# A graph network kernel: the last group's scatters spread between chunks, and the first chunks' fetches moved, in its second layer

## The chip, the cores and the metric

One core of a Trainium2 chip runs the whole program in one launch. The core has five engines with queues of their own: TensorE (PE: matmuls; PEld is its loading of weights), VectorE (DVE), ScalarE (ACT), GpSimd (POOL) and SyncE (SP), which here only starts transfers. The metric is the device time of one execution in microseconds (us), lower is better. All data are 32-bit floats.

## The reference

The model is a stack of four layers, each `x = x + layer(relu(layernorm(x)))`, on x of 128 x 64 x 256. Layer 0 is two graph convolutions and an LSTM, layer 2 a convolution with two batch norms, layer 3 a dense graph attention. The change lies in layer 1, an attention over 512 edges of a graph with 64 nodes and 4 heads:

```python
Xq = (H @ W_lin.T).reshape(bt, n, h, dh)
Xv = (H @ W_val.T).reshape(bt, n, h, dh)
Qs = Xq[:, src]
Kt = Xq[:, dst]
e = jnp.einsum('behd,hd->beh', jax.nn.leaky_relu(Qs + Kt, LRELU_SLOPE), a)
e = e + jnp.log(A0[src, dst] + EPS)[None, :, None]
...
attn = ex / denom[src]
...
Y = jax.ops.segment_sum(attn[..., None] * Vt, src, num_segments=n)
...
return Y @ W_out.T
```

The softmax runs over the edges that share a source node.

## The kernel before

The 8192 tokens (128 x 64) are cut into 16 chunks of 512 (`NCH`), and these into 4 groups of 4 chunks (`NGR`; a group is 2048 tokens). Layer 1 runs in two stretches.

The edge loop, `edges(q)` for q from 0 to 31, takes two tiles of 128 tokens per step: `gather` (line 959) forms query sums for all edges with a matmul, ScalarE copies them out of the accumulation banks, VectorE applies the leaky ReLU (971), `project` (940) makes the queries and values of the tiles to come, `score` (974) adds each edge's score into the group's bank. A group has its scores after eight steps. Its softmax, `edge_softmax(g)` (990), is a generator. `step_behind` (1171) advances it by one `yield`, and `edges` calls this three times per step, so that a group's softmax is spread over some six steps of the next group.

The parts of `edge_softmax`, in order: scores plus log weights (993), two scans for the maximum (996, 998), subtraction and exponential (1002, 1003), two scans for the sums (1006, 1008), four reciprocals (1013), the product (1015), four transposes on TensorE (1019), the multiplication by `twins` into `attn` (1024). Then eight scatters from GpSimd (1058), one for each half of the partitions (`par`) and block of 128 edges (`ec`), write rows of attention to a field of 64 x 64 in DRAM. `part_back` (1039) brings the field back into the tile `dense[g]`, in two loads or, for the last group, in four.

From step 25 on, every second step also calls `values_of(n)` (1188) for n = 0 to 3. Behind the loop it runs for n = 4 to 15 (1285), and this is the second stretch, the chunk loop. `values_of(n)` calls `weigh(n)` (64 small matmuls of 64 x 64, line 1122, and a copy on ScalarE), `fetch(n + 2)` (values `xv` from DRAM, but for the last four chunks, which stay on chip; and the chunk `xo` of x), `turn_attention(n + 2)` (one copy of `dense` on ScalarE and one on VectorE, line 1104), the store of chunk n - 2, and `put_out(n - 1)` (16 matmuls, line 1142, and two additions to x, 1152). Unless `hold` is set it then calls `sums` (1156) for chunks that are put out: sums for the next layer's norm on VectorE, and four small operations on GpSimd for the roots. For n = 0 it first fetches and turns chunks 0 and 1. Chunks 12 to 15 are those of the last group, so chunk 12's attention (`LAST`) is turned only at n = 11.

The last group's softmax has no edge steps left to hide behind. Four parts of it run at the end of step 31, seven ahead of n = 4, and the rest, from the transposes on, in one go ahead of n = 6.

The order in each engine's queue is set at build time by a scheduler that may move an instruction ahead of others that it takes to be ready later. `late(ins)` pins an instruction behind the one traced before it on its engine. `add_manual_dep` with `Sync` makes an instruction wait for another one.

Buffers that matter: four accumulation banks (`bank`), two double banks (`pair_bank`), three `att`, three `xv`, four `xo`, four of each small statistics tile. `l1` is the layer's scope.

Of the kernel before, what the change touches and what calls it, by code (L numbers as in the profile page):

```python
# [12 lines left out]
AF = mybir.ActivationFunctionType  # L13
ALU = mybir.AluOpType
# [16 lines left out]
def gnn_stack_kernel(ctx: ExitStack, tc: tile.TileContext, a: dict, out: bass.AP):  # L31
# [11 lines left out]
    def bank():  # L43
        return psums["now"].tile([P, 512], F32, tag="bank", name="bank", bufs=psums["banks"])
# [26 lines left out]
    def late(ins):  # L71

        tc.keep_in_program_order(ins)
# [805 lines left out]
    with ExitStack() as l1:  # L879
# [110 lines left out]
        def edge_softmax(g):  # L990

            e = e1.tile([P, E], F32, tag="e", name="e")
            late(nc.vector.tensor_tensor(e, scores[g], logw, ALU.add))
            run = e1.tile([P, E], F32, tag="run", name="run")
            yield
            late(nc.vector.tensor_tensor_scan(run, first, e, NEG, ALU.add, ALU.max))
            yield
            late(nc.vector.tensor_tensor_scan(
                run[:, ::-1], final[:, ::-1], run[:, ::-1], NEG, ALU.add, ALU.max
            ))  # L1000
            yield
            late(nc.vector.tensor_tensor(e, e, run, ALU.subtract))
            late(nc.scalar.activation(e, e, AF.Exp))
            yield

            late(nc.vector.tensor_tensor_scan(run, keep, e, 0.0, ALU.mult, ALU.add))
            yield
            late(nc.vector.tensor_tensor_scan(
                run[:, ::-1], final[:, ::-1], run[:, ::-1], NEG, ALU.add, ALU.max
            ))  # L1010
            yield
            for k in range(NE):
                late(nc.vector.reciprocal(run[:, k * P : (k + 1) * P], run[:, k * P : (k + 1) * P]))
                yield
            late(nc.vector.tensor_tensor(e, e, run, ALU.mult))
            yield
            p = bank()
            for ec in range(NE):
                ins = nc.tensor.transpose(p[:, ec * P : (ec + 1) * P], e[:, ec * P : (ec + 1) * P], ident)
                if ec == 0 and g == NGR - 1:  # L1020
                    late(ins)
            yield
            attn = e1.tile([P, NE, P], F32, tag="attn", name="attn")
            late(nc.vector.tensor_tensor(
                attn,
                p.rearrange("p (e r) -> p e r", e=NE),
                twins.unsqueeze(2).to_broadcast([P, NE, P]),
                ALU.mult,
            ))

            sent = [[], []]

            dense[g] = attp.tile([P, T, T], F32, tag="dense", name="dense")

            def bring_back(par, parts=1):
                for k in range(parts):
                    part_back(par, k, parts)

            def part_back(par, k, parts):

                r, s = slice(par * T, (par + 1) * T), slice(k * 32 // parts, (k + 1) * 32 // parts)
                back = nc.gpsimd.dma_start(
                    out=dense[g][r, :, :].rearrange("p (o s) r -> p o s r", o=2)[:, :, s, :],
                    in_=fields1[2 * g + par][: T * T, :].rearrange("(t o s) r -> t o s r", t=T, o=2)[
                        :, :, s, :
                    ],
                )
                for ins in sent[par]:
                    tc.add_manual_dep(
                        back.ins,  # L1050
                        ins.ins.name,
                        mybir.DependencyInfo(mybir.DependencyClass.Sync, mybir.DependencyReason.DATA),
                        reason="rows of the field",
                    )

            for par in range(2):
                for ec in range(NE):
                    ins = nc.gpsimd.indirect_dma_start(
                        out=fields1[2 * g + par][:, :],
                        out_offset=bass.IndirectOffsetOnAxis(ap=row_of[:, ec : ec + 1], axis=0),  # L1060
                        in_=attn[:, ec, par * T : (par + 1) * T],
                        in_offset=None,
                    )
                    for earlier in sent[par]:
                        tc.declare_no_dep(ins.ins, earlier.ins, reason="different rows")
                    sent[par].append(ins)
                    if ec % 2:
                        yield
            if g == NGR - 1:

                for k in range(2):
                    for par in range(2):
                        part_back(par, k, 2)
            else:
                bring_back(0)
                yield
                bring_back(1)
# [33 lines left out]
        def weigh(n):  # L1111

            (xv, xt), att = fetched.pop(n), turned.pop(n)
            yT = yp.tile([P, 8, 2, T], F32, tag="yT", name="yT")
            p = pair_bank()
            for c in range(2):
                for i in range(4):
                    for h2 in range(2):
                        for par in range(2):
                            r = slice(par * T, (par + 1) * T)  # L1120
                            hd = 2 * c + h2
                            ins = nc.tensor.matmul(  # L1122
                                p[h2 * T : (h2 + 1) * T, par, (c * 4 + i) * T : (c * 4 + i + 1) * T],
                                xv[r, i, hd * T : (hd + 1) * T],
                                att[r, i % 2, i // 2 * 4 + hd, :],
                                start=True,
                                stop=True,
                            )
                            if c + i + h2 + par == 0:
                                late(ins)  # L1130
            nc.scalar.copy(
                yT.rearrange("p k o t -> p o k t"), p.rearrange("p o (k t) -> p o k t", t=T)
            )
            return xt, yT
# [18 lines left out]
            stores.append((n, xt))  # L1153
            unnormed.append((n, xt))

        def sums(n, xt):

            st = stat.tile([P, 4, 6], F32, tag="ln_st", name="ln_st")
            mv = stat.tile([P, 4, 2], F32, tag="ln_mv", name="ln_mv")
            for i in range(4):  # L1160
                nc.vector.bn_stats(st[:, i, :], xt[:, i, :])
                nc.vector.bn_aggr(mv[:, i, :], st[:, i, :])
            rs, nm = x_rs[:, n, :], x_nm[:, n, :]
            nc.gpsimd.tensor_scalar(rs, mv[:, :, 1], 1e-5, None, ALU.add)
            nc.gpsimd.tensor_tensor(rs, rs, half_power, ALU.pow)
            nc.gpsimd.tensor_tensor(nm, mv[:, :, 0], rs, ALU.mult)
            nc.gpsimd.tensor_scalar(nm, nm, -1.0, None, ALU.mult)
# [14 lines left out]
                step_behind()  # L1182

        NT = NTOK // P
        dense, fetched, turned, weighed, stores, unnormed = {}, {}, {}, [], [], []
        LAST = NCH - 4

        def values_of(n, hold=False):

            if n == 0:  # L1190
                for k in range(2):
                    fetch(k)
                    turn_attention(k)
            one = (n, *weigh(n))
            if n + 2 < NCH:
                fetch(n + 2)
            if n == LAST:
                turn_attention(n + 1)
            if n + 2 < NCH and not LAST <= n + 2 < LAST + 2:
                turn_attention(n + 2)  # L1200
            flush_stores()
            flush_values()

            if n + 1 == LAST:
                turn_attention(LAST)
            weighed.append(one)
            if not hold:
                while unnormed:
                    sums(*unnormed.pop(0))

        def flush_stores():
            while stores:
# [7 lines left out]
        def next_score():  # L1220
            q, c, lrs = waiting.pop(0)
            score(q, c, lrs)
            if q % 8 == 7 and c == 1:
                behind.append(edge_softmax(q // 8))

        def edges(q):
# [20 lines left out]
                sums1(n + 3, (0, 1))  # L1247
            while len(waiting) > (1 if q < NT // 2 - 1 else 0):
                next_score()

        coming1 = {n: load_x1(n) for n in (2, 3)}
        hTs[0] = t1.tile([P, 2, CHUNK], F32, tag="hT1", name="hT1")
# [32 lines left out]
        for n in range(4, NCH):  # L1285
            if n == 4:
                for _ in range(7):
                    step_behind()
            if n == 6:
                finish_behind()  # L1290
            values_of(n, n in (4, 5))
            if n - 10 in first_x2:
                scale_x(n - 10, first_x2.pop(n - 10))
        flush_stores()
# [631 lines left out]
```

## Time and profile before

| what | us |
|---|---|
| median of 3 runs | 2091.2 (2090.15 to 2093.34) |
| the profiled execution | 2088.75 |
| its span | 2086.8 |
| layer 1 in it, about | 1300 to 1697 |
| its edge loop, about | 1308 to 1619 |
| its chunk loop (chunk 4 on) | 1624 to 1695 |

The profile shows one execution. Its page gives each engine's busy time and share of the span, the busy share in 40 slices, and the clock that TensorE was granted. Views of the trace give more: the chain of waits follows the work that ended last back from its end; the timeline lists instructions in order of time, with the idle time before them and what ended it; the windows give busy time by stretch. "issue" is time in which an engine waited for nothing that the profile shows. On GpSimd, DMA_INDIRECT is a scatter and DMA_DIRECT2D a plain transfer.

### The profile page before, as it was taken

The page shows a single profiled execution, that of the slowest core. Times are in us where ns is not written, and L with a number is a line of the kernel's source. Part 1 is how long each engine was busy: PE and PEld are TensorE (multiplying, and loading weights), DVE is VectorE, ACT ScalarE, POOL GpSimd, SP SyncE. Part 2 cuts the span into 40 slices and gives each one's busy share as a digit, 9 for nine tenths or more (in the row PEclk, how much of TensorE's full clock was granted, in tenths as well). Part 3 has the DMA queues.
Part 4 walks back from the last instruction along what each step waited for, and adds up shares of the span by engine and source line. Part 5 has one row for each costly group of instructions (what it writes and reads, how often), then busy time and mean ns, then how long its engine had stood idle before and what let it go on. Part 6 is the DMA issues. An engine that isn't in the chain of part 4 may idle for free.

```text
span 2086.8 us, 25504 instructions
## 1 busy us (share of the span) xinstructions
PE 2016.4 (97%) x9444; PEld 1353.1 (65%) x9444; DVE 1362.5 (65%) x2509; ACT 1180.1 (57%) x2222; POOL 317.7 (15%) x422
## 2 busy tenths in 40 slices
PE   8999999999999999999999998999999999999998
PEld 6776488766688746886667885333334775444786
DVE  8764766564655577557446555676766767786776
ACT  4344766554555467566546553666665356592444
POOL 3000010100200020002001002114322420000563
PEclk9999999999999999999999999999999999999899
DMA  9331000100100250001001006113234851023012
GB/s 310 98 96 51 0 21 1 41 0 1 41 1 1 89 194 21 1 1 41 1 0 41 1 1 227 61 51 96 75 82 117 257 186 59 0 71 91 31 61 71
DMA packets 94461, 135.06 MB, mean 65 GB/s; under 512 B 6401, under 2 KB 82049, under 8 KB 92161
## 3 DMA queue, kind: packets, MB, share of 16 engines
q1 hardware_dynamic: 87616, 109.11, 15.9%
q0 software_dynamic: 6112, 24.12, 3.9%
q8 instruction: 74, 1.21, 0.2%
q14 instruction: 51, 0.41, 0.1%
q10 hardware_dynamic: 608, 0.20, 0.1%
HBM read 87.28 MB, written 46.14 MB: 64 GB/s over the span
## 4 chain that ended last, share of the span: by engine, by line
PE 85%; DVE 7%; ACT 3%; DMA 2%; issue 1%; POOL 1%; SPq 0%; ACTq 0%; POOLq 0%; DVEq 0%
PE pa L643 25%; PE pc L643 13%; PE bank L50 12%; PE pb L643 6%; PE pa L1361 5%; PE pair L964 5%; PE bank L948 5%; PE bank L1142 3%; PE bank L980 2%; PE pc L1361 2%; PE pb L1361 1%; PE pair L50 1%; ACT gate L671 1%; PE pair L1122 1%; PE bank L167 1%
## 5 line engine op out<-in xcount | busy, mean ns | idle before, releaser
L643 PE MATMUL pa<-xop,sih 128*128 128x256 f32 (+2 forms) x1056 | 343.9, 417 | 11.3 <-DVE gate L697 7.7
L671 ACT ACTIVATE gate<-gate,bias 128x256 f32<-128x256 f32 (+2 forms) x368 | 247.4, 679 | 172.4 <-DVE gate L687 89.1
L643 PEld LDWEIGHTS pa<-xop,sih 128*128 128x128 f32 x1056 | 198.2, 190 | 86.6 <-issue 22.2
L643 PE MATMUL pc<-xop,wih 128*128 128x256 f32 (+2 forms) x736 | 251.2, 423 | 0.0
L687 DVE TENSOR_TENSOR gate<-pb,gate 128x256 f32<-128x256 f32 (+2 forms) x184 | 87.4, 475 | 224.3 <-PE pb L643 152.6
L643 PE MATMUL pa<-lstm_h,shh 128*128 128x256 f32 (+1 forms) x672 | 212.7, 398 | 0.0
L971 DVE SCALAR_TENSOR_TENSOR lr<-lr 128x1024 f32<-128x1024 f32 x128 | 150.3, 1217 | 64.5 <-ACT lr L970 58.3
L643 PEld LDWEIGHTS pc<-xop,wih 128*128 128x128 f32 x736 | 139.8, 190 | 51.2 <-issue 23.0
L702 DVE TENSOR_TENSOR gate<-pc,gate 128x256 f32<-128x256 f32 (+2 forms) x184 | 87.6, 476 | 119.5 <-PE pc L643 119.2
L970 ACT COPY lr<-pair 128x1024 f32<-128x1024 f32 x128 | 123.1, 1013 | 48.8 <-PE pair L964 46.2
L643 PEld LDWEIGHTS pa<-lstm_h,shh 128*128 128x128 f32 x672 | 127.7, 190 | 30.2
L643 PE MATMUL pc<-lstm_h,whh 128*128 128x256 f32 (+1 forms) x448 | 141.8, 398 | 0.0
L686 ACT COPY gate<-pa 128x256 f32<-128x256 f32 (+2 forms) x184 | 76.0, 413 | 96.2 <-PE pa L643 95.8
L964 PE MATMUL pair<-sd_hot,xq 64*128 64x512 f32 x512 | 128.0, 618 | 2.3 <-ACT lr L970 2.3
L948 PE MATMUL bank<-wlv,hT 128*128 128x512 f32 x256 | 118.4, 605 | 0.2 <-ACT hT L156 0.2
L697 DVE TENSOR_TENSOR gate<-pa,gate 128x256 f32<-128x256 f32 (+2 forms) x184 | 87.3, 475 | 44.0 <-PE pa L643 43.4
L691 ACT COPY gate<-pa 128x256 f32<-128x256 f32 (+2 forms) x184 | 75.5, 410 | 59.0 <-PE pa L643 57.6
L671 ACT ACTIVATE gate<-pa,bias 128x256 f32<-128x256 f32 (+2 forms) x184 | 93.9, 510 | 25.9 <-PE pa L643 24.3
L434 POOL TENSOR_TENSOR sih<-wih 128x512 f32<-128x512 f32 x8 | 10.6, 1325 | 626.1 <-DMA wih<-in_WihT 438.9
L643 PE MATMUL pa<-xop,wih 128*128 128x256 f32 (+1 forms) x320 | 101.4, 398 | 2.6 <-ACT xop L624 2.6
L643 PE MATMUL pb<-xop,wih 128*128 128x256 f32 (+1 forms) x320 | 100.3, 398 | 0.4 <-DVE gate L687 0.4
L643 PEld LDWEIGHTS pc<-lstm_h,whh 128*128 128x128 f32 x448 | 85.1, 190 | 20.1
(337 smaller groups left out, 3824.4 us busy)
## 6 DMA issues: line engine op xcount, KB each, us to landing
field<-sd_hot SPq DMA_DIRECT2D x8, 1152.0 KB, 11.2
wih<-in_WihT SPq DMA_DIRECT2D x8, 1024.0 KB, 6.4
xres<-in_x SPq DMA_DIRECT2D x16, 512.0 KB, 5.5
xa<-xres POOLq DMA_DIRECT2D x16, 512.0 KB
xin<-xb SPq DMA_DIRECT2D x16, 512.0 KB, 3.9
h<-xb SPq DMA_DIRECT2D x16, 512.0 KB, 3.9
xin<-in_x SPq DMA_DIRECT2D x15, 512.0 KB, 7.0
out_x<-h SPq DMA_DIRECT2D x15, 512.0 KB, 2.9
```

Of the source, the lines that this page charges most:

```text
L50: nc.tensor.matmul(o, lhsT, rhs, start=start, stop=stop)
L643: ins = nc.tensor.matmul(p[:, : self.N], weights[kind, self.phase](k, q), x[k], start=first_ and kind == "ih", stop=kind == "hh" or not se ...
L671: nc.scalar.activation(out, in_, AF.Tanh if q == 2 else AF.Sigmoid, bias=bias[:, self.w - 1, 2 * q + j : 2 * q + j + 1],)
L686: nc.scalar.copy(blk[0, 0], pa[:, :N])
L687: nc.vector.tensor_tensor(blk[0, 0], pb[:, :N], blk[0, 0], ALU.add)
L697: nc.vector.tensor_tensor(blk[1, 1], pa[:, :N], blk[1, 1], ALU.add)
L702: nc.vector.tensor_tensor(blk[1, 0], pc[:, :N], blk[1, 0], ALU.add)
L948: ins = nc.tensor.matmul(p, hTs[n][:, k, i * P : (i + 1) * P], wlv[:, k, :], start=k == 0, stop=k == 1)
L964: ins = nc.tensor.matmul(p[:, par, :], queries[it][r, c * P : (c + 1) * P], sd_hot[r, :], start=True, stop=True)
L970: nc.scalar.copy(lr, p)
L971: nc.vector.scalar_tensor_tensor(lr, lr, 0.2, lr, ALU.mult, ALU.max)
L1361: ins = nc.tensor.matmul(p, lhs[k], x[k], start=first_, stop=last_one, skip_group_check=True)
```

## The change

The softmax of groups 0 to 2 gets one more step between product and transposes, and its transposes are pinned. For the last group, the multiplication by `twins` moves from one VectorE operation to four on ScalarE, one for each block of 128 edges; transposes and multiplication form one step, and the scatters follow in batches of three, three and two, each scatter waiting for the last matmul of the latest weighting (`last_weigh`). The four loads of the last group's field are pinned behind the scatters. These steps are now called ahead of n = 6 and inside `values_of` for n = 6, 7 and 8, right behind `weigh`. The `sums` are held for n = 4 to 7 (before: 4 and 5), then called for two chunks at a time; for n = 8, 9 and 10 their first GpSimd operation is pinned, so that it comes behind the scatters and loads. The fetches and attention copies of chunks 0 and 1 move from `values_of(0)`, behind step 25, to the end of step 23.

```diff
             late(nc.vector.tensor_tensor(e, e, run, ALU.mult))
             yield
+            if g < NGR - 1:
+                yield
             p = bank()
             for ec in range(NE):
                 ins = nc.tensor.transpose(p[:, ec * P : (ec + 1) * P], e[:, ec * P : (ec + 1) * P], ident)
-                if ec == 0 and g == NGR - 1:
+                if ec == 0:
                     late(ins)
-            yield
+            if g < NGR - 1:
+                yield
             attn = e1.tile([P, NE, P], F32, tag="attn", name="attn")
-            late(nc.vector.tensor_tensor(
-                attn,
...
+            if g == NGR - 1:
+                for ec in range(NE):
+                    late(nc.scalar.activation(
+                        attn[:, ec, :],
+                        p[:, ec * P : (ec + 1) * P],
+                        AF.Identity,
+                        scale=twins[:, ec : ec + 1],
+                    ))
+            else:
+                late(nc.vector.tensor_tensor(
+                    attn,
...
+                if g == NGR - 1:
+                    late(back)
                 for ins in sent[par]:
...
+            if g == NGR - 1:
+                yield
             for par in range(2):
                 for ec in range(NE):
                     ins = nc.gpsimd.indirect_dma_start(
...
                     sent[par].append(ins)
-                    if ec % 2:
+                    if g == NGR - 1:
+
+                        tc.add_manual_dep(
+                            ins.ins,
+                            last_weigh[0].ins.name,
+                            mybir.DependencyInfo(mybir.DependencyClass.Sync, mybir.DependencyReason.DATA),
+                            reason="weights first",
+                        )
+                        if len(sent[0]) + len(sent[1]) in (3, 6):
+                            yield
+                    elif ec % 2:
                         yield
...
+            last_weigh[0] = ins
             nc.scalar.copy(
                 yT.rearrange("p k o t -> p o k t"), p.rearrange("p o (k t) -> p o k t", t=T)
             )
...
-        def sums(n, xt):
+        def sums(n, xt, keep=False):
...
-            nc.gpsimd.tensor_scalar(rs, mv[:, :, 1], 1e-5, None, ALU.add)
+            ins = nc.gpsimd.tensor_scalar(rs, mv[:, :, 1], 1e-5, None, ALU.add)
+            if keep:
+                late(ins)
...
         def values_of(n, hold=False):
 
-            if n == 0:
-                for k in range(2):
-                    fetch(k)
-                    turn_attention(k)
             one = (n, *weigh(n))
+            if n in (6, 7):
+                step_behind()
+            elif n == 8:
+                finish_behind()
...
             if not hold:
-                while unnormed:
-                    sums(*unnormed.pop(0))
+                for _ in range(2 if n > 6 else 4):
+                    if unnormed:
+                        sums(*unnormed.pop(0), 8 <= n < 11)
...
             while len(waiting) > (1 if q < NT // 2 - 1 else 0):
                 next_score()
+            if q == NT // 2 - 9:
+                for k in range(2):
+                    fetch(k)
+                    turn_attention(k)
...
             if n == 6:
-                finish_behind()
-            values_of(n, n in (4, 5))
+                step_behind()
+            values_of(n, 4 <= n < 8)
```

More of the change, by code (lines that the diff above doesn't have):

```diff
@@ L1019, in edge_softmax @@
                 ins = nc.tensor.transpose(p[:, ec * P : (ec + 1) * P], e[:, ec * P : (ec + 1) * P], ident)
[L1020 removed]
+                if ec == 0:
                     late(ins)
[L1022 removed]
+            if g < NGR - 1:
+                yield
             attn = e1.tile([P, NE, P], F32, tag="attn", name="attn")
[L1024 to L1029 removed]
+            if g == NGR - 1:
[9 more added lines that the diff above has]
+                    attn,
+                    p.rearrange("p (e r) -> p e r", e=NE),
+                    twins.unsqueeze(2).to_broadcast([P, NE, P]),
+                    ALU.mult,
+                ))
             sent = [[], []]
@@ L1184, in gnn_stack_kernel @@
         NT = NTOK // P
+        last_weigh = [None]
         dense, fetched, turned, weighed, stores, unnormed = {}, {}, {}, [], [], []
```

## The prediction, made before the changed kernel was built or run

> **What bounds the kernel now.** I read the page first.
>
> ```profile
> span 2086.8 us, 25504 instructions
> PE 2016.4 (97%) x9444; PEld 1353.1 (65%) x9444; DVE 1362.5 (65%) x2509; ACT 1180.1 (57%) x2222; POOL 317.7 (15%) x422
> ...
> PEclk9999999999999999999999999999999999999899
> ```
>
> TensorE is busy for 97% of the span, so this change, which takes no matmul away, can win only where TensorE stands idle or runs at a lower clock. There are some 70 us of idle time, and I looked for the part of it in layer 1 (about 1300 to 1700 us). The timeline of TensorE, with the idle time before each row in brackets, shows three places in the edge loop:
>
> ```profile
> 1414.78 0.63 PE L1019 MATMUL bank<-ident,e 128*128 128x128 f32 x4 [0.75 <-DVE e L1015]
> ...
> 1494.21 0.63 PE L1019 MATMUL bank<-ident,e 128*128 128x128 f32 x4 [0.75 <-DVE e L1015]
> ...
> 1546.54 0.34 PE L1122 MATMUL pair<-att,xv_in 64*64 64x64 f32 x8 [1.50 <-ACT att L1104]
> 1549.80 1.77 PE L1122 MATMUL pair<-att,xv_in 64*64 64x64 f32 x56 [2.91 <-DVE att L1104]
> 1551.49 2.65 PE L964 MATMUL pair<-sd_hot,xq 64*128 64x512 f32 x8
> ```
>
> Twice the transposes of a group's softmax wait 0.75 us for VectorE's product (A). Once the first weighting, chunk 0, waits for its two attention copies, 1.50 and 2.91 us (B). The row after B takes 2.65 us where such a row takes 1.92 elsewhere: the clock was lower.
>
> The chain of waits then shows the chunk loop at the end of layer 1:
>
> ```profile
> 1638.71 1.09 PE pair L1122 x64
> 1639.81 3.65 PE bank L1142 x16
> 1643.46 0.73 PE pair L1122 x39
> ...
> 1649.07 0.98 issue
> ...
> 1651.49 5.57 PE bank L1142 x16
> 1657.06 1.09 PE pair L1122 x64
> 1658.15 3.65 PE bank L1142 x16
> ...
> 1671.32 1.08 ACT att L1104
> 1672.40 0.04 issue
> 1672.44 1.17 PE pair L1122 x64
> ```
>
> A chunk is a weighting of 1.09 and an output product of 3.65 us. Chunk 8's weighting starts at 1643.46 and its successor at 1651.49: 8.03 us for 1.09, with pauses of 0.3 to 1 us that no semaphore explains ("issue"), and the next product takes 5.57 instead of 3.65 (C). At 1671.3 chunk 12, the first of the last group, waits for its attention copy (D, 1.16 us idle).
>
> GpSimd's timeline says what stands beside C and ahead of D:
>
> ```profile
> 1642.74 0.96 POOL L1058 DMA_INDIRECT field<-attn,row_of  x1 [0.30 <-issue]
> 1644.00 1.34 POOL L1058 DMA_INDIRECT field<-attn,row_of  x1 [0.30 <-issue]
> ...
> 1649.43 0.96 POOL L1058 DMA_INDIRECT field<-attn,row_of  x1 [0.30 <-issue]
> 1650.47 0.67 POOL L1042 DMA_DIRECT2D dense<-field  x1
> 1655.72 1.75 POOL L1042 DMA_DIRECT2D dense<-field  x3 [4.58 <-DMA field<-attn,row_of]
> ```
>
> The eight scatters run from 1640.03 to 1650.39, a pitch of 1.26 us. TensorE's pauses begin 0.9 us into chunk 8's weighting and end a microsecond after the last scatter. The output products beside the first three scatters ran at 3.65 us: 32 instructions in that time can be fed, 128 in 1.09 us cannot. The last three loads of the field are issued by 1657.47 and chunk 12's copy starts 13.85 us later: that is their way through the DMA engines, which the windows of the stages show nearly full:
>
> ```profile
> 1643.00:1657.00 14.00, 9.70 (x86) 6.78 (x84) 6.72 (x22) 1.98 (x2) 7.81 (x10) 0.76 0.90 301
> 1657.00:1672.00 15.00, 14.28 (x241) 11.93 (x240) 11.03 (x33) 6.67 (x9) 13.38 (x29) 1.00 0.82 199
> ```
>
> (Columns: length, the five engines, clock, DMA share, GB/s.) The clock of 0.76 is the price that C goes on paying.
>
> [...] the clock falls behind gaps that add to 4.4 and some 5 us. [...] the row of 0.96 us is followed by 4.58 us of waiting. [...]
>
> **The change, part by part.** Times are the profiled execution's: 2088.75 us, span 2086.8; the shown runs' median, 2091.2, lies 2.45 above it. I subtract savings from both alike.
>
> A: groups 0 to 2 get one more step between product and transposes. VectorE's product is done long before; the transposes then stand behind the next gather. Saves 2 x 0.75 = 1.5. All later steps of a group (attention, eight scatters, two field loads) move one step too; group 2's field is first copied for chunk 8, some 20 us later, so nothing waits. Bounds 0 to 1.5.
>
> B: the fetches and four attention copies of chunks 0 and 1 move from behind step 25 to behind step 23. From 1545.03 to 1554.14 TensorE needs 9.11 us for one weighting and one gather, 1.09 + 1.92 = 3.01 elsewhere: 6.1 too many, clock included. Kept: some 0.3, since the gather's second tile needs the bank that chunk 0's copy (1.01 us) empties. Saves 5.8. At the new place ScalarE gets two copies of 1.08 us; it idled 0.64 and 0.89 us there around 1526 to 1529, so its gather copies come up to 1.5 us late and it catches up within the step; TensorE needs those banks only 4 us later. VectorE's two copies of 0.6 fit its gaps of 1 to 2.4 us. Four loads move on SP's queue; their buffers' stores are two steps old. If the cover fails: 1.5 lost.
>
> C: three scatters after the weighting of chunk 6, three after 7, two after 8, each batch waiting for the weighting's last matmul. Behind them on GpSimd are only the later scatters, the field loads and the roots of deferred sums. Attention goes from one VectorE row (0.68) to four activations of 128x128 on ScalarE. Nearest rows: two-pointer 128x256 activations start 0.50 apart, and 512 against 256 columns (0.59, 0.37) give 0.11 for 128 columns: 4 x 0.39, about 1.5, bounds 1.0 to 1.8. The only thing delayed is chunk 6's copy out of its bank. Three scatters take 3 x 1.26 = 3.8 against a product of 3.65: the next weighting overlaps a batch by 0.2 to 0.8, and chunk 8 got 39 matmuls before it starved. I take 0.3 for each of two weightings, bounds 0 and 1.5. Saves 6.94 + 1.92 - 0.6 = 8.3 ahead of chunk 12.
>
> D: what is late next. Chunk 6's weighting stood at 1633.97; six chunks of 4.745 later, plus 0.6, chunk 12 is due at 1663.0. The last batch starts when chunk 8's weighting ends, 1645.15, and is generated by 1647.7. Landing took 5.3 us after the last scatter here, 1.75 in group 2 on quiet engines: I take 3.5, 1651.2. Three loads of 0.58: 1653.0. Then 13.85 as before, 1666.8, and the copy: chunk 12 starts at 1668.0, only 4.4 earlier than 1672.44, after a wait of 5 us that halves the clock again (about 1.5, as in B). C and D together: 2.9. Best: 1.75, and 2.1 MB at 199 GB/s, 10.5: 1662.8, no wait, 9.4. Worst: 5.3 and 17 us: 1672.9 and 3 of clock, -3.
>
> Deferred sums: six chunks of 2.1 us of VectorE work come behind chunk 8, two per chunk. 2 x 2.1 + 2 x 0.69 + 0.6 = 6.2 against 4.75 for five chunks: 7 us behind; banks and output buffers allow one chunk's delay. I take 0, since VectorE may fill earlier gaps, bounds 0 to 2.3.
>
> Sum: 1.5 + 5.8 + 2.9 = 10.2 us; span 2076.6, time 2091.2 - 10.2 = 2081.0.
>
> **The rivals.** R1: the field lands in time (fewer loads compete, since the last four chunks' values are kept on chip; against it stands the DMA share of 0.8 to 0.9): 1.5 + 5.8 + 9.4 = 16.7, 2074.5. R2: the tail gives nothing, for the field lands as late as before and the clock pays 1.5: 5.8, 2085.4. For it: the fetch on SP already waited up to 13.6 us for a store behind these loads. R3, slower: TensorE's feed doesn't recover between batches, so that the weightings of chunks 7, 8 and 9 (line 1122) each pay what chunk 8 paid: 3 x 8.86 = 26.6 instead of 8.86, D's 1.2 hidden, A and B kept: 26.6 - 8.9 - 1.2 - 7.3 = +9.2, 2100.4. For it: scatters beside an output product precede each, as before chunk 8. Against it: the pauses ended 1.1 us after the last scatter. It decides if recovery takes over about 6 us. R4: A and B are eaten by the worst ends of D and of the sums, 7.3 - 3 - 2.3 = 2: 2089.2.
>
> **How the numbers follow.** Forecast 0.40, R1 0.15, R2 0.18, R4 0.10, R3 0.17. A measurement of this kernel can tell about 0.2%, 4.2 us, from no change. Faster: the first three less 0.02 for their edges, 0.71; within: 0.12; slower: 0.17. The forecast's own range is 2077 to 2085; 2072 to 2094 leaves out R3 and little else.
>
> **What would show it.** A: no idle before line 1019. B: a weighting of 1.1 us at step 25 at full clock. C: batches of three scatters, each beginning at a weighting's end, and weightings of 1.1 to 1.6. D: chunk 12 waiting about 5 us for the field. Weightings of several microseconds beside scatters, or idle time in the edge loop behind step 23, would make me wrong.

## The result, and the profile after

| | before | after |
|---|---|---|
| median of 6 runs, us | 2091.1 (2089.0 to 2093.3) | 2078.8 (2078.0 to 2083.0) |
| the profiled execution | 2088.75 | 2079.25 |
| its span | 2086.8 | 2077.5 |

The ratio is 0.9943 (95%: 0.993 to 0.9955): 12.4 us less between the medians, 9.3 us less between the two profiled spans. The forecast was 2081.0, in a range of 2077 to 2085 of its own and of 2072 to 2094 with all rivals but R3.

The page shows that TensorE's busy time fell by only 2.7 us (2016.4 before) for the same 9444 matmuls, so what went is idle time, and time at a lower granted clock. The windows show 0.50 from 1549.5 to 1552.9 (behind B) and from 1648.5 to 1655.3 (C) in before, and in after once in this layer, from 1652.4 to 1659.2.

```profile
span 2077.5 us, 25503 instructions
...
PE 2013.7 (97%) x9444; PEld 1350.0 (65%) x9444; DVE 1359.9 (65%) x2508; ACT 1180.2 (57%) x2226; POOL 315.7 (15%) x422
```

TensorE's timeline of after, at the three places of A and B (start, duration, instruction; idle time before it in brackets):

```profile
1418.79 0.66 PE L1021 MATMUL bank<-ident,e 128*128 128x128 f32 x4
...
1497.23 0.66 PE L1021 MATMUL bank<-ident,e 128*128 128x128 f32 x4
...
1544.05 1.16 PE L1148 MATMUL pair<-att,xv_in 64*64 64x64 f32 x64
1545.14 2.33 PE L964 MATMUL pair<-sd_hot,xq 64*128 64x512 f32 x8
1547.40 3.70 PE L948 MATMUL bank<-wlv,hT 128*128 128x512 f32 x8
```

No bracket is left: the two waits of 0.75 us before the transposes are gone (A), and chunk 0's 64 matmuls run in one piece in 1.16 us instead of waiting 1.50 and 2.91 (B). The row behind them, which took 2.65 at a granted clock of 0.74, takes 2.33 at 1.00.

The chunk loop, in the same view. Line 1148 is the weighting (1122 before), 1169 the output product (1142 before):

```profile
1631.20 1.18 PE L1148 MATMUL pair<-att,xv_in 64*64 64x64 f32 x64
1632.32 3.72 PE L1169 MATMUL bank<-wout,yT 128*128 128x256 f32 x16
1635.97 1.16 PE L1148 MATMUL pair<-att,xv_in 64*64 64x64 f32 x64
...
1654.41 1.99 PE L1148 MATMUL pair<-att,xv_in 64*64 64x64 f32 x64 [4.15 <-DMA xv_in<-xv]
1656.33 5.11 PE L1169 MATMUL bank<-wout,yT 128*128 128x256 f32 x16
1661.37 0.34 PE L1148 MATMUL pair<-att,xv 64*64 64x64 f32 x8
1663.82 1.04 PE L1148 MATMUL pair<-att,xv 64*64 64x64 f32 x56 [2.11 <-DVE att L1130]
1664.80 3.72 PE L1169 MATMUL bank<-wout,yT 128*128 128x256 f32 x16
1668.45 1.16 PE L1148 MATMUL pair<-att,xv 64*64 64x64 f32 x64
...
1686.98 3.93 PE L50 MATMUL bank<-bdH,h 128*128 128x128 f32 x32 [0.78 <-DVE xo_last L1179]
```

The weightings of chunks 7 and 8 (first and third row) show no pause: C is gone. (Where the text below says that such a weighting takes 0.94 us, it counts from the start of its first matmul to the start of its last; the row counts to the end, 1.16. The profile lists 64 matmuls for the 32 in the code of `weigh`, and 16 for the 8 of `put_out`.) But chunk 11, at 1654.41, now waits 4.15 us for its values and runs at a lower granted clock (0.50 from 1652.4 to 1659.2; 1.99 and 5.11 us for 1.16 and 3.72), and chunk 12 is split by a wait of 2.11 us for VectorE. GpSimd's timeline of after:

```profile
1628.45 1.12 POOL L1074 DMA_INDIRECT field<-attn,row_of  x1 [23.83 <-ACT attn L1029]
...
1633.15 0.96 POOL L1074 DMA_INDIRECT field<-attn,row_of  x1 [0.91 <-PE pair L1148]
...
1637.44 0.96 POOL L1074 DMA_INDIRECT field<-attn,row_of  x1 [0.80 <-PE pair L1148]
...
1645.39 1.75 POOL L1054 DMA_DIRECT2D dense<-field  x3 [4.59 <-DMA field<-attn,row_of]
```

And ScalarE's:

```profile
1660.18 1.08 ACT L1130 COPY att<-dense 128x512 f32<-128x512 f32 x1 [2.65 <-DMA dense<-field]
```

Where the text speaks of generation, it means such a row on GpSimd; the transfer itself lands later: the last scatter's row ends at 1639.66, and the three loads wait for the scatters' landing until 1645.39. The scatters stand in batches of three, three and two; the second and third wait for a weighting, as they should. The last three loads of the field are issued by 1647.14, and ScalarE's copy for chunk 12 starts when they have landed, 13.04 us later. Until then nothing that TensorE does earlier helps chunk 12. The windows show how busy the DMA engines are ahead of that way and on it (length, the five engines, clock, DMA share, GB/s):

```profile
1634.00:1643.00 9.00, 9.00 (x160) 7.53 (x159) 8.61 (x21) 3.48 (x5) 4.61 (x6) 1.00 1.04 337
1643.00:1657.00 14.00, 9.85 (x158) 8.28 (x157) 6.05 (x22) 4.45 (x8) 10.71 (x21) 0.83 1.03 244
```

TensorE is some 7 us ahead here. For the same part of the work the DMA share was 0.91 and 0.97 in the kernel before (1641.44 to 1650.44 and 1650.44 to 1664.44): the DMA engines were nearly full already, and they are full now.

Where the 9.3 us between the spans are, from the starts of rows in both timelines: 8.5 from the start of the edge loop to chunk 6's weighting (325.89 to 317.40); 1.3 from there to chunk 13's (43.29 to 41.99); minus 1.0 from chunk 13's weighting to the second row of line 50 (22.66 to 23.70); 1.6 in the layers behind. The edge loop itself began 1.0 later, which comes off. What the layers behind give differs from run to run, since stretches at a granted clock of 0.50 fall differently there (3.4 us from 1832.8 and 13.7 from 1928.3 before, 10.2 from 1922.0 after), and the change doesn't touch them.

### The profile page after: what moved, and what is told of

It is laid out like the page before. It is cut to its first block, busy times and chain, and to the rows that moved or that the text cites. A ratio compares the mean times of both kernels' runs of the same rounds, so it can differ in the third digit from the quotient of the medians.

```text
span 2077.5 us, 25503 instructions
## 1 busy us (share of the span) xinstructions
PE 2013.7 (97%) x9444; PEld 1350.0 (65%) x9444; DVE 1359.9 (65%) x2508; ACT 1180.2 (57%) x2226; POOL 315.7 (15%) x422
## 4 chain that ended last, share of the span: by engine, by line
PE 87%; DVE 6%; ACT 3%; DMA 2%; issue 1%; POOL 1%; ACTq 0%; POOLq 0%; DVEq 0%; SPq 0%
PE pa L643 25%; PE bank L50 13%; PE pc L643 13%; PE pb L643 6%; PE pair L964 6%; PE bank L948 5%; PE pa L1396 5%; PE bank L980 3%; PE bank L1169 3%; PE pc L1396 2%; PE pb L1396 1%; PE pair L50 1%; ACT gate L671 1%; PE pair L1148 1%; PE bank L167 1%
```

## The experiments

All times are medians in us, beside runs of the kernel before in the same session, on the same chip. e4_plain is a single time.

| run | what it is | time | before | ratio (95%) |
|---|---|---|---|---|
| e1_edge | A and B alone | 2086.4 | 2090.9 | 0.9979 (0.9972 to 0.9986) |
| e2_tail | the rest alone | 2090.0 | 2090.9 | 0.9998 (0.9989 to 1.0006) |
| e3_nowait | the change without the scatters' wait | 2090.3 | 2090.9 | 1.0002 (0.999 to 1.0013) |
| e4_plain | before, plain transfers for scatters | 2090.2 | 2090.9 | |
| e5_hold | e1, group 2's scatters held | 2081.3 | 2091.2 | 0.9956 (0.994 to 0.9973) |
| e6_xv | the change, chunk 11's load early | 2085.7 | 2091.2 | 0.9977 (0.9969 to 0.9985) |
| e7_both | e6, inputs 9 to 12 without waits | 2086.8 | 2091.2 | 0.9985 (0.9976 to 0.9994) |
| e8_all | e7, field in two tiles (and along another axis) | 2087.3 | 2091.2 | 0.9981 (0.9973 to 0.9989) |
| e9_after | the change again | 2079.1 | 2088.5 | 0.995 (0.9933 to 0.9966) |
| e10_after_hold | the change, group 2's scatters held | 2078.1 | 2088.5 | 0.9947 (0.993 to 0.9963) |
| e11_xv_hold | e10 and e6's early load | 2079.4 | 2088.5 | 0.9953 (0.9937 to 0.997) |
| e12_again | the change a third time | 2080.4 | 2091.9 | 0.9945 (0.9928 to 0.9962) |

**The two halves: e1_edge and e2_tail.** e1 puts only this into the kernel before (A and B); e2 takes just this out of the kernel after:

```diff
+            if g < NGR - 1:
+                yield
             p = bank()
...
-                if ec == 0 and g == NGR - 1:
+                if ec == 0:
...
-            if n == 0:
-                for k in range(2):
-                    fetch(k)
-                    turn_attention(k)
...
+            if q == NT // 2 - 9:
+                for k in range(2):
+                    fetch(k)
+                    turn_attention(k)
```

> The kernel before with the two edge-loop edits alone (one more step and pinned transposes for groups 0 to 2; first fetches and attention copies behind step 23). If the gain is made in the edge loop and the tail gives nearly all back: 7.5 to 9 us faster than before, the chunk loop still pausing about 7 us at chunk 8 and 1.2 us at chunk 12. If the edits' gain depends on the tail (the tail earns most of the 12 us): 3 to 5 us faster at most.

> The changed kernel with the two edge-loop edits undone, so the tail's edits alone. If the tail gives back what it wins: 0 to 4 us faster than before, with no pause at chunk 8 and waits at chunks 11 and 12 that add to 6 us or more. If the tail earns on its own: 6 to 9 us faster.

e1 gave 4.5 us and e2 0.9, which can't be told from nothing: 5.4 together, where the whole change gave 12.4. The parts don't add up, and the traces say what is missing. In e1 the edge loop gains as it should up to chunk 2's weighting, which then takes this course (TensorE's timeline of e1, weighting at line 1124):

```profile
1588.81 1.29 PE L1124 MATMUL pair<-att,xv_in 64*64 64x64 f32 x44
1590.50 0.35 PE L1124 MATMUL pair<-att,xv_in 64*64 64x64 f32 x4 [0.40 <-issue]
1591.24 0.35 PE L1124 MATMUL pair<-att,xv_in 64*64 64x64 f32 x5 [0.39 <-issue]
1591.97 0.36 PE L1124 MATMUL pair<-att,xv_in 64*64 64x64 f32 x6 [0.38 <-issue]
1592.72 0.37 PE L1124 MATMUL pair<-att,xv_in 64*64 64x64 f32 x5 [0.40 <-issue]
1593.49 3.61 PE L1144 MATMUL bank<-wout,yT 128*128 128x256 f32 x16 [0.40 <-issue]
```

Forty-four matmuls go in 1.29 us and then four to six every 0.73 us. No semaphore ends the pauses. It is the picture of chunk 8 before, at a new place: A moved every later step of a group by one, so that group 2's scatters, whose first began 3.8 us ahead of chunk 2's weighting in the kernel before (1592.7 and 1596.51), begin 1.8 us ahead of it (1586.97 and 1588.81). In the kernel before the third scatter (1595.39 to 1597.02) and the beginning of the fourth lie beside that weighting and cost it one pause of 0.32 us; in e1 it is the second to the fifth. The step from chunk 2's weighting to chunk 3's is 27.32 us in e1, 21.96 in the kernel after: 5.4 lost. In e2 the weightings of chunks 7 and 8 each show one pause beside a batch of three (0.95 and 0.93 us longer than in after): 1.9 lost. 5.4 + 1.9 = 7.3, which is about what the halves lack (12.4 - 5.4 = 7.0). In the kernel after, the scatters stand at the same places beside chunk 2 (1587.81, 1589.23, 1590.51 against a weighting from 1589.65) and it doesn't starve. So e1's time fits the second of its two expected cases, 3 to 5 us, but not for its reason: what is missing was lost at chunk 2 and isn't earned at the end of the layer. e2's time fits its first case, except for the pauses at chunks 7 and 8.

**What starves: e3_nowait and e4_plain.** e3 leaves out the wait of the last group's scatters for a weighting, and so runs them in one row:

```diff
-                        tc.add_manual_dep(
-                            ins.ins,
-                            last_weigh[0].ins.name,
...
```

> The changed kernel without the scatters' wait for the latest weighting; nothing else is changed and the results stay the same. If scatter generation beside a weighting starves TensorE, the eight scatters run in one go from about 1628.5 and the weightings of chunks 7 and 8 take several us each instead of 1.1 (5 to 12 us of pauses in all); the field comes 2 us sooner. If what mattered was where the sums and the field loads stand, the weightings stay at 1.1 to 1.6 us and the time is the changed kernel's within 2 us.

e4 is the kernel before with eight plain transfers of the same size in place of the last group's scatters. So the last group's attention comes to stand in other rows:

```diff
-                    ins = nc.gpsimd.indirect_dma_start(
...
+                    if g == NGR - 1:
+                        ins = nc.gpsimd.dma_start(
+                            out=fields1[2 * g + par][ec * P : (ec + 1) * P, :],
+                            in_=attn[:, ec, par * T : (par + 1) * T],
+                        )
```

> The kernel before with plain transfers from GpSimd, of the same bytes, in place of the last group's eight scatters, so that its attention lands in the wrong rows of the field. If it is the generating of scatters that starves TensorE, the pauses at chunk 8 are gone (weighting below 1.6 us) although the DMA engines move the same bytes. If it is DMA traffic that starves it, chunk 8 still takes 5 us or more.

In e3 the eight scatters run from 1632.02 to 1642.06, and chunk 7's weighting (TensorE's timeline, line 1142) falls to one to three matmuls at a time:

```profile
1636.64 0.33 PE L1142 MATMUL pair<-att,xv_in 64*64 64x64 f32 x2
1637.82 0.31 PE L1142 MATMUL pair<-att,xv_in 64*64 64x64 f32 x2 [0.85 <-issue]
...
1642.83 0.26 PE L1142 MATMUL pair<-att,xv_in 64*64 64x64 f32 x1 [0.34 <-issue]
1643.56 1.62 PE L1142 MATMUL pair<-att,xv_in 64*64 64x64 f32 x49 [0.47 <-issue]
```

It takes 8.2 us, and the other 49 matmuls go through in 1.6, from 1.5 us after the last scatter is generated. That is the first theory's case, but for chunk 8: its weighting, expected to suffer too, comes when the scatters are over and is whole. e4's plain transfers are generated in 4.38 us from 1640.51 (GpSimd's timeline), and chunk 8's weighting is whole (TensorE's, line 1128):

```profile
1644.08 1.16 PE L1128 MATMUL pair<-att,xv_in 64*64 64x64 f32 x64
```

The first theory expected that. But e4 doesn't separate a scatter's generation from its bytes as it was meant to: the transfers' packets move from 1644.94 to 1648.82, nearly all beside the output product that follows, and their generation lies beside only the first 0.81 us of the weighting, where the kernel before had no pause either (its pauses began after 0.9). Two other traces say more. In e3 no packet of the scatters moved from 1636.62 to 1640.04, while GpSimd was generating scatters and TensorE got matmuls by ones to threes. In e7 all scatters and the first load were generated by 1644.06, and chunk 9's weighting, from 1644.48, is whole, though packets of the scatters still move beside it and the DMA share is 1.09. And e7's chunk 10 pauses for 0.88 us beside the generation of three plain loads (TensorE's timeline of e7, then GpSimd's):

```profile
1644.48 1.16 PE L1152 MATMUL pair<-att,xv_in 64*64 64x64 f32 x64
...
1649.22 1.16 PE L1152 MATMUL pair<-att,xv_in 64*64 64x64 f32 x62
1651.25 0.33 PE L1152 MATMUL pair<-att,xv_in 64*64 64x64 f32 x2 [0.88 <-issue]
...
1643.39 0.67 POOL L1054 DMA_DIRECT2D dense<-field  x1
1650.32 1.75 POOL L1054 DMA_DIRECT2D dense<-field  x3 [6.25 <-DMA field<-attn,row_of]
```

So in these traces the pauses go with the generation of transfers on GpSimd, and not with the bytes on the DMA engines; that plain transfers do it too rests on the one place in e7, and in the kernel after the same three loads stood beside chunk 10's weighting (1645.39 and 1645.45) without a pause. e4 also says, as far as one run can, what C is worth alone: nothing. Without any pause at chunk 8 its chunk 12 starts 38.2 us after chunk 6, against 38.5 before; chunk 11 waits instead.

**The lost part of the edge half: e5_hold.** e1, with group 2's eight scatters two steps later and held until a weighting is done:

```diff
+            for _ in range(2 if g == NGR - 2 else 0):
+                yield
             for par in range(2):
...
+                    if g == NGR - 2:
+                        tc.add_manual_dep(
+                            ins.ins,
+                            last_weigh[0].ins.name,
...
```

> The edge part alone (A and B, no change at the end of the layer), and group 2's eight scatters held until the weighting of chunk 2 is done. Theory 1, what is missing of the edge part's gain was lost because these scatters, now one step earlier, stand beside the weighting of chunk 2: that weighting takes 0.94 us instead of 4.07, the step from it to chunk 3's falls from 27.3 to about 22 us, and the time is 3 to 5.4 us below the edge part alone (2086.4), 2081 to 2083.5, ratio to before about 0.996. Theory 2, the edge part's gain is lost at the end of the layer, where the transfers set the end: the weighting of chunk 2 is short, but chunks 8 to 13 wait longer, and the time stays at 2085 to 2088.

The weighting of chunk 2 is whole, the step to chunk 3 is 21.96, and the time is 9.8 below before instead of 4.5. The first theory held. What A and B are worth when nothing starves is thus most of what the whole change gives; in e5 the last group's scatters still starve chunk 8, whose matmuls start over 5.4 us instead of 0.94.

**The end of the layer: e6_xv, e7_both, e8_all.** Chunk 11 waits for its values because its load is issued late: SP stands at the load of an input that waits for a store, 6.5 us (1635.36 + 0.75 to 1642.62 in SP's timeline), and only then, at 1643.77, issues this one. e6 loads the values before chunk 5, into a buffer that is free after the edge loop, and e7 puts four inputs into such buffers too:

```diff
+            if n == 5:
+                early_xv[11] = spare()
+                nc.sync.dma_start(out=early_xv[11], in_=xv_mem[11])
...
-            if n < NCH - 3:
+            if 9 <= n < NCH - 3:
+                xt = spare()
+            elif n < NCH - 3:
```

> The changed kernel with the values of chunk 11 loaded before chunk 5, into a buffer that is free after the edge loop; nothing else. Theory 1, chunk 11's load is late because it stands on SP's queue behind a load that waits for a store: chunk 11's wait of 4.15 us goes, and with it most of the low clock behind it; then chunk 12 waits for the field, which lands at about 1660, and 2 to 4 us are left of the gain, 2075 to 2077. Theory 2, the transfers' rate alone sets when chunk 12 can start, and the time of chunk 12's weighting is as before (about 1661 to 1664): under 1 us gained, 2078 to 2080, and chunk 12 waits instead of chunk 11.

> As the run before it, and the inputs of chunks 9 to 12 go into buffers that are free after the edge loop, so that their loads wait for no store. Theory 1, order on the queues: no wait on SP for a store, chunk 10's input is there in time, VectorE doesn't stand at that addition and copies chunk 12's attention as soon as the field lands; the waits of chunks 11 and 12 (4.15, 2.11) go, a wait for the field's last load of up to 3 us stays: 2072 to 2075. Theory 2, the transfers' rate: the same bytes are in the way, the loads land no sooner, and the time is within 1.5 us of the changed kernel's, 2077 to 2080.

> As the run before it, and the last group's field is read into two tiles, so that the attention of chunks 12 and 13 waits for its own two loads and not for all four. Theory 1: the two first loads land some 3 us before the last one, so chunk 12 starts up to 3 us sooner and waits for nothing, or under 1 us; full clock throughout; 2069 to 2073. Theory 2, the transfers' rate: within 1 us of the run before it.

e8's edit also takes the attention along another axis of the field, in all 16 chunks, so that they weigh with other parts of it. In the kernel after each of the last four chunks needs rows of all four loads, so its first copy can't go ahead on two. e8's time is within half a microsecond of e7's, and nothing more is read from it.

None of the three is faster than the change, and e6 and e7 looked slower, 5.5 and 4.4 below before, where both theories had expected 11 or more. But both starved at chunk 2 (3.9 and 4.0 us) and at chunks 7 and 8 (1.8 to 1.9 each), though they differ from the kernel after only from chunk 5 on. Hence the last four runs.

**Program or chip: e9_after, e10_after_hold, e11_xv_hold, e12_again.** e9 and e12 are the changed kernel itself. e10 is the changed kernel with e5's edit, e11 is e10 with e6's.

> The changed kernel itself once more, beside kernels that are compared with it. In its first profile the weighting of chunk 2 took 0.94 us between scatters, while every kernel that has parts of the change took about 4 us there when the scatters stood so; so did the changed kernel with one load moved, behind that place. Theory 1, it is the program (where its instructions and queues come to lie): 0.94 us again, 2077 to 2082. Theory 2, it is the chip or the session: about 4 us for chunk 2, some 1.9 for chunks 7 and 8, and 2084 to 2087.

> The changed kernel with group 2's scatters held until the weighting of chunk 2 is done. If the changed kernel starves at chunk 2 on this chip, this takes 3 to 5 us off it. If it doesn't, the two are within 1 us of each other. The weighting of chunk 2 takes 0.94 us in either case.

> As the run before it, and chunk 11's values loaded before chunk 5, as in e6_xv. Theory 1, order on SP's queue: 2 to 4 us below e10_after_hold. Theory 2, the field's landing sets chunk 12: within 1 us of e10_after_hold, chunk 11 waits for nothing, and chunk 12's weighting starts 33.5 to 35 us after chunk 6's, as in e6_xv and e7_both.

> The changed kernel a third time. So far the kernels of the first two calls (labels e1 to e8) starved at the weighting of chunk 2 or at those of chunks 7 and 8 wherever scatters stood beside them, and those of the third call (e9 to e11), on another chip, did not. Theory 1, it is the program: 0.94 us at chunk 2 and under 1 us at chunks 7 and 8 on this chip too, 2077 to 2081. Theory 2, it is the chip: on a chip that starves, about 4 us at chunk 2, 1.9 at chunks 7 and 8, and 2084 to 2087; on one that doesn't, as theory 1.

The changed kernel didn't starve in either run, with 0.94 us at chunk 2 and 0.94 to 0.97 at chunks 7 and 8, and gained 9.5 and 11.5 us. So the result repeats. What decides whether a weighting starves beside scatters that stand the same way is not settled. The sessions ran on different chips: e1 to e8, which starved wherever scatters stood beside a weighting, on two; e9 to e11 on a third and e12 on a fourth, where none did. e3, e6 and e7 are written as the kernel after up to chunk 2, and starved there. This leans to the chip or the session, but no changed kernel was profiled on chips of both kinds, and the times of the kernel before (2090.9, 2091.2, 2088.5 and 2091.9 in the four sessions) don't decide it. It also bounds the result: where e6 and e7 ran, the change with small edits gained only 4.4 to 5.5 us, and what the changed kernel itself would gain there was not measured.

With the starving gone, e11 tells about chunk 11's load. TensorE's timeline (weighting at line 1156), with ScalarE's copy:

```profile
1650.03 1.16 PE L1156 MATMUL pair<-att,lr_spare 64*64 64x64 f32 x64
1651.12 3.72 PE L1177 MATMUL bank<-wout,yT 128*128 128x256 f32 x16
1658.78 0.34 PE L1156 MATMUL pair<-att,xv 64*64 64x64 f32 x8 [3.93 <-ACT att L1138]
1661.99 1.77 PE L1156 MATMUL pair<-att,xv 64*64 64x64 f32 x56 [2.87 <-DVE att L1138]
...
1657.66 1.06 ACT L1138 COPY att<-dense 128x512 f32<-128x512 f32 x1 [5.33 <-DMA dense<-field]
```

Chunk 11 no longer waits at all, and chunk 12 waits instead, for the copy that waits for the field. The time is within noise of e10's (2079.4 and 2078.1). The second theory held in what chunk 12 waits for, and in that no time was won; its numbers were missed by a little (1.3 us apart instead of 1, and chunk 12 comes 32.48 us after chunk 6, not 33.5 to 35). In fact chunk 12 starts 3.1 us sooner after chunk 6 than in e10, and all of it is given back behind it. With chunk 11's load from SP's queue out of the way, the last loads of the field, from GpSimd's queue, took 10.39 us from issue to ScalarE's copy, against 13.36 in e10.

The starts of the weightings of chunks 6, 12 and 13 put it together:

| kernel | 6 to 12, us | 12 to 13 | 6 to 13 |
|---|---|---|---|
| before | 38.54 | 4.75 | 43.29 |
| after | 34.91 | 7.08 | 41.99 |
| e9_after | 33.35 | 8.98 | 42.33 |
| e12_again | 34.36 | 6.52 | 40.88 |
| e10_after_hold | 35.61 | 6.26 | 41.87 |
| e11_xv_hold | 32.48 | 9.60 | 42.08 |
| e6_xv | 33.72 | 10.28 | 44.00 |
| e7_both | 35.07 | 9.25 | 44.32 |
| e2_tail | 34.85 | 8.99 | 43.84 |
| e4_plain | 38.18 | 5.97 | 44.15 |
| e3_nowait | 41.23 | 6.16 | 47.39 |

Where the change's batches run, chunk 12 comes 2.9 to 6.1 us sooner after chunk 6 than before, and 1.5 to 5.5 of them are given back before chunk 13: a lower clock behind the waits takes a part (in e11 the windows show 0.77 from 1657 to 1672), and the order on VectorE the rest. In after, the copy that lets chunk 12's last 56 matmuls go stands behind the two additions of chunk 10, the ones traced just before it, behind which `late` pins it (VectorE's timeline):

```profile
1660.20 0.61 DVE L1130 COPY att<-dense 128x512 f32<-128x512 f32 x1 [1.72 <-DMA dense<-field]
1661.00 0.69 DVE L1179 TENSOR_TENSOR xo<-bank,xo 128x512 f32<-128x512 f32 x1 [0.19 <-DMA xo<-xa]
...
1662.61 0.66 DVE L1179 TENSOR_TENSOR xo<-bank,xo 128x512 f32<-128x512 f32 x1
1663.18 0.58 DVE L1130 COPY att<-dense 128x512 f32<-128x512 f32 x1
```

The first addition's input landed just then, but that is not the cause: in e7 and e11 it was there, and TensorE waited 2.73 and 2.87 us at this place all the same. What holds the additions back in e7 is the deferred `sums` (VectorE's timeline of e7):

```profile
1658.27 0.25 DVE L1193 BATCH_NORM_AGGREGATE ln_mv<-ln_st 128x2 f32<-128x6 f32 x2 [2.59 <-POOL x_nm L1199]
...
1660.30 0.38 DVE L1193 BATCH_NORM_AGGREGATE ln_mv<-ln_st 128x2 f32<-128x6 f32 x4 [1.05 <-POOL x_nm L1199]
1662.33 0.25 DVE L1193 BATCH_NORM_AGGREGATE ln_mv<-ln_st 128x2 f32<-128x6 f32 x2 [1.64 <-POOL x_nm L1199]
...
1663.97 0.69 DVE L1183 TENSOR_TENSOR lr_spare<-bank,lr_spare 128x512 f32<-128x512 f32 x1
```

VectorE stands three times for GpSimd's roots of earlier sums (`x_nm`), whose small tiles are to be used again, and comes to chunk 10's first addition only when the field has landed. The kernel before has one such wait here, of 1.51 us; after has 2.58, 1.04 and 1.65. That chunk 12's copy would go sooner without them is argued and not shown. Another order on VectorE was not tried, and no run beat the changed kernel by more than the measurement can tell (e10: 1.0 us below e9).

## Why the prediction was right, point by point

The forecast's main case came true: the edge loop gives most, the end of the layer little, since the field's landing takes the place of chunk 8's pauses.

- **Step A**, 1.5: from the edge loop's start to the scoring (line 980) ahead of chunk 0's weighting the changed kernel needs 233.14 us instead of 235.10, 2.0 less. The two waits were 1.5 of it; the other 0.5 was not traced to a place.
- **Step B**, 5.8: from that scoring to line 948 behind the weighting, 5.20 instead of 10.97: 5.77. This term was right to a few hundredths. The moved copies and loads cost nothing that shows.
- **"All later steps of a group ... move one step too ... so nothing waits", bounds 0**: the step that was wrong. The field came in time, as said, but the scatters' own neighbour had changed. The step from chunk 2's weighting to chunk 3's went from 22.54 to 21.96 in the changed kernel, a gain of 0.6, and to 27.3 in e1 and e3, a loss of 4.8. The profile of before had a warning that I had read at chunk 8 only, in TensorE's timeline at the end of chunk 2's weighting:

```profile
1596.51 1.04 PE L1122 MATMUL pair<-att,xv_in 64*64 64x64 f32 x56
1597.88 0.38 PE L1122 MATMUL pair<-att,xv_in 64*64 64x64 f32 x8 [0.32 <-issue]
```

  A pause that no semaphore explains, beside the same group's scatters.
- **Step C**, 8.3 ahead of chunk 12: from chunk 6's weighting to chunk 9's it was 23.08 us before and is 14.25, so 8.8 were won there, and D took most of it back. The pauses at chunk 8 in the profile before add to 4.2 us, not to some 5. The new activations took 1.14 us (1.5 taken) and loaded no table: both traces have seven table loads, none of them at this line. The residual of 0.3 per weighting, bounds 0 to 1.5: 0 in the changed kernel, 0.8 to 1.0 each in e2, e6 and e7. If the bounds are for the two weightings together, these runs are above them.
- **Step D**: taken at 7.3 us earlier for A and B, the working had the last batch at 1637.85 (it was 1637.44), chunk 12's copy at 1659.5 (1660.18) and its weighting at 1660.7 (1661.37). So the sum of generation, landing and loads came out well, but two of its terms were off and cancelled in part: the landing took 5.7 us from the last scatter to the loads (3.5 taken), and the loads' way 13.04 (13.85). Three things looked different. The wait fell on chunk 11, which has its own late load, and e11 shows that this hid the wait for the field. The granted clock of 0.50 behind the wait, counted as 1.5, cost 2.2 at chunk 11 (6.96 us to chunk 12 for 4.74). And behind chunk 12 the copy on VectorE cost 2.3 more, in no term of the sum (4.75 to 7.08 from chunk 12 to 13). C and D gave 1.3 instead of 2.9; in e9 and e12 1.0 and 2.4.
- **Deferred sums**, 0, bounds 0 to 2.3: likely more than 0. They stand in the order on VectorE for which TensorE waits 2.11 us at chunk 12, as the lines of e7 show; how much of it is theirs was not measured.
- **Not in the sum**: the first row of line 50 behind the layer waits 0.78 us for VectorE's last addition, and the stretch from chunk 13 to the second such row is 23.70 or 23.71 us in all eleven traces that have A and B, and 22.65 or 22.66 in the three that don't (before, e2, e4). So the edge half costs 1.0 at the end of the layer. The likely reason, argued and not shown, is that a moved step turns the rotation of the accumulation banks, so that line 50 takes the bank that is emptied last.

Edge loop 8.5 for 7.3, end of the layer 1.3 for 2.9, and 1.0 against: 8.8 of a forecast 10.2. The medians' 12.4 and the repeats' 9.5 and 11.5 lie around it. That the total came out so near is in part luck: the errors have both signs, some 1.6 us between the profiles lie in layers that the change doesn't touch, and the moved scatters of group 2, taken at nothing, cost nothing only in the sessions in which the changed kernel ran; in e6, which differs from it by one load, they cost 5.1 at chunk 2.

R1 fell: chunk 12's copy on ScalarE waited for the field in every run of the change. R2 was close, since e2 shows that the new end of the layer gives nothing alone; it paired with a smaller edge half than there was. R3's stall is real, and decides more than its chance of 0.17 said: with chunks 2 and 7 starving, e3 has lost all of the gain, and in e1 the stall took 5.4 us from the edge half. But R3 as put, three weightings that each pay what chunk 8 paid, was not seen: with batches of three the weightings of chunks 7 and 8 paid 0.8 to 1.0 each at most. Its condition was put wrongly. What counted in these runs is not a recovery time between batches but whether GpSimd was generating transfers while one of these weightings ran (8.2 us for chunk 7 in e3, with chunk 8 whole behind the last scatter), and something more that these runs don't name.

## What to carry to other kernels

Before moving a step, list what it issues and what will stand beside each of those instructions at the new place. Eight scatters that cost nothing beside large matmuls (21.96 us from chunk 2 to 3 in e5) cost 5.4 us beside 64 small ones (27.32 in e1), in some sessions. When a stall goes and the time stays, look for the transfer that the next stage waits for. A load that shows as the last wait can hide another that ends just as late, and only a run without the first tells. And halves that don't add up in a split are worth a look at the traces, since the rest may lie at a place that neither half was meant to touch.

## What was not expected of the hardware

- While GpSimd generated scatters (1.26 us apart), TensorE got 4 to 6 small matmuls per 0.73 us, after 44 in 1.24 to 1.29 us at the start (chunk 2 in e6 and e1); in one long row of scatters it fell to 1 to 3 (chunk 7 in e3). The pauses went with generation on GpSimd and not with the packets on the DMA engines (e3: pauses while no packet of the scatters moved, from 1636.62 to 1640.04; e7: a whole weighting at a DMA share of 1.09), and once they stood beside the generation of plain loads (0.88 us in e7). What holds the matmuls back was not shown.
- Two programs that are written alike up to a place, with scatters at the same distance, starved and didn't: 3.93 us (e6) and 0.94 us (after, three times). So the working's "128 in 1.09 us cannot" is what chunk 8 showed, and no rule. Program or chip is open.
